# Attention stream: filled-in products in thirds, seven PSUM banks in one set, and a new order of a unit's steps

## The chip, the cores and the metric

The kernel runs on one core of a Trainium2 chip. The metric is the device time of one execution in microseconds. Three runs of the kernel before took 5718.77, 5719.36 and 5725.56 us, so the median is 5719.36 us.

## The reference

The program is a two-part encoder on x of shape (4, 2048, 256), float32 throughout.

- Part 1: `x = x + attention(layernorm(x))`. Full self-attention with 16 heads of 16 features over all 2048 positions, separately for each of the 4 batches: `softmax(Q K^T / 4 + lambda * prior) V`, then an output projection. The prior depends on the distance d of the two positions alone: `0.8 exp(-(d-1)^2/0.5) + 0.4 exp(-(d-30)^2/8)`, which the kernel takes as zero from a distance of 60 on.
- Part 2: `x = x + two local layers(layernorm(x))`. Each has windowed attention (8 heads of 64, window 128, rotary positions) and a gated feed-forward network.

The change lies in part 1, the "attention stream".

## The kernel before

**Units.** The stream has 1024 units: 4 batches x 16 heads x 16. In its first stage a unit u takes 128 queries of a head against all 2048 keys, for the largest score of every query. In its second stage, LEAD = 22 units later, a unit s takes 128 keys against all 2048 queries with the maximum already in the product, and makes exponentials and the weighted sum of values. The loop over t emits for each t the steps of `ORDER`, a list written out by hand: stage one of unit t and stage two of unit t - 22, interleaved. A prime after a step's name (`m'`) means that it is done for the unit before (t - 1). TensorE (PE), ScalarE (ACT) and VectorE (DVE) execute their instructions in just this order; while t < LEAD the shorter list `FIRST` is used.

**Steps of a unit.** Scores have 512 columns each; four make a unit in either stage. A *half* is one of the two halves of the keys; it has a left and a right score tile.

- `L`, `R` (L866): the two left and the two right products of stage one. In `R`, where a half is not touched by the prior's band (it is not `apart`), the keys are the difference right minus left (`kd`), so that max(left, right) = left + relu(difference).
- `r` (L886, ACT): relu of such a difference. `m` (L890, DVE): the maximum of left plus relu. One half of a unit is of this kind in 14 of 16 units, none in the other two.
- `dR`, `dL` (L878 plain maximum, L880 with the prior added; DVE): the maxima of a half's right and left tile where the half is `apart`. L880 is two rows of the profile, the operation and a READ_ACCUMULATOR.
- `A`, `B` (L949): two products each of stage two. `bA`, `bB` (L960, DVE): the prior's band added to the tiles that it touches. `x0` to `x3` (L964, ACT): the four exponentials, `x0` and `x1` of `A`'s tiles, `x2` and `x3` of `B`'s.
- `W` (L973): the weighted sums, eight rows of PE. `W'` takes the exponentials of the unit before.
- `F` and `E`: places for filled-in work. At most one filled-in group of products goes to PE in a unit, at `F`; what reads its result comes at `E`.

**Filled-in work.** A timetable of generators (`fillers`) runs two slots per unit, one at `F` and one at `E`. `on_pe()` yields until it is at an `F` that nobody has taken. The generators are: `projections` of the following batch (per group of four chunks: two transposes `xt`, four products `pqk` of 6 matmuls, two `pv` of 12 matmuls of half the width), `residual` of the batch before (eight transposes `oT`, eight groups `ao` of 12 matmuls), and `prepare_layers`, which prepares weights of part 2 and has 20 small groups `b_w`; it pauses while one of the other two is active (`counted`, `when_quiet`). `projections(b)` starts at unit (b-1)*256 + 60, `residual(b)` at unit (b+1)*256 + 25.

**PSUM.** Eight banks. One holds the weighted sums of a head (`pacc`). Stage one has a pool of its own of three banks (`P1 = 3`), for four tiles per unit. Stage two and the filled-in products share the other four. A product waits until the instructions that read the tile before it in its bank are done.

**DVE work per head.** Four short steps of `negated` (L898 to L909) at the steps in `BETWEEN`, and the steps of `kept_sums` (two transposes L984 and L989, a copy on ACT, a reciprocal) at `R` and `dR`.

Of the kernel before, what the change touches and what calls it, by code (L numbers as in the profile page):

```python
# [37 lines left out]
P = 128  # L38
# [22 lines left out]

ORDER = "m' R A F r dR bA x0 B E L bB x2 W' dL x1 x3".split()

FIRST = "m' R r dR bA L bB F dL E x3".split()

BETWEEN = "bA", "bB", "dL", "x3"

# [5 lines left out]
SECOND, TURN = 12, 8  # L73
PART, FULLS, MORE, P1 = 2, 4, 2, 3
Q_BUFS, V_BUFS = 6, NC + 2
# [112 lines left out]
def encoder_kernel(  # L188
# [47 lines left out]

    def prepare_layers(wp, psum, on_pe, behind):

# [21 lines left out]
        for l in range(DEPTH):  # L260
# [66 lines left out]
            for k in range(2):  # L327
                rows = l_w1[l, k * P : (k + 1) * P, :]
                for at, n in ((0, 3), (3, 2), (FULL, 3), (FULL + 3, 2), (2 * FULL, 1)):
# [20 lines left out]
                    yield from behind()  # L350
                    nc.vector.tensor_tensor(b1[:, at : at + n], b1[:, at : at + n], ps[:, :n], ALU.add)
                    nc.gpsimd.tensor_scalar(s, s, lb[:, 0, k : k + 1], None, ALU.mult)
                    yield
# [45 lines left out]

    def dense(ps, lefts, rights, last=True, first=True):  # L400

        n = len(lefts)
        for k in range(n):
            (lh, ll), (rh, rl) = lefts[k], rights[k]
            for i, (a, c) in enumerate(((lh, rh), (lh, rl), (ll, rh))):
                nc.tensor.matmul(  # L406
                    ps, a, c, start=first and k == 0 and i == 0,
                    stop=last and k == n - 1 and i == 2,
                )

# [17 lines left out]
    def attention():  # L428
        with ExitStack() as es:
# [8 lines left out]
            xp = es.enter_context(tc.tile_pool(name="ax", bufs=2))  # L438
            p1 = es.enter_context(tc.tile_pool(name="p1", bufs=P1, space=PSUM))
            p2 = es.enter_context(tc.tile_pool(name="p2", bufs=7 - P1, space=PSUM))  # L440
            pacc = es.enter_context(tc.tile_pool(name="pa", bufs=1, space=PSUM))

            def psum(name):
                return p2.tile([P, 512], F32, tag="ps", name=name)

# [113 lines left out]
            xts, keys = {}, {}  # L559
            phase = {"at": None, "taken": False}  # L560

            def on_pe():

                while phase["at"] is not None and (phase["at"] or phase["taken"]):
                    yield 1
                phase["taken"] = True

            def behind():
# [29 lines left out]
            def turned(b, g, xt):  # L598
                t = xts[b, g] = [
                    xp.tile([P, 2, QT], F32R, tag=f"xT{i}", name=f"xT{i}_{b}_{g}", bufs=XT_BUFS)  # L600
                    for i in range(2)
                ]
                for k in range(2):
                    yield from on_pe()
                    ps = psum(f"xt_{b}_{g}_{k}")
                    for i in range(4):
                        nc.tensor.transpose(
                            ps[:, i * P : (i + 1) * P], xt[:, i, k * P : (k + 1) * P], ident
                        )
                    yield from behind()  # L610
                    nc.scalar.copy(t[0][:, k], ps)
                    yield 1
                    nc.vector.tensor_tensor(t[1][:, k], ps, t[0][:, k].bitcast(F32), ALU.subtract)

            def store(queue, stack, cols, part, parts):
# [11 lines left out]
            def project_qk(b, i, m, g, given=None):  # L627
# [6 lines left out]
                feats = slice(m * P, (m + 1) * P)  # L634
                dense(
                    ps,
                    [[w[:, a, i, k, feats] for a in range(2)] for k in range(2)],
                    [[xT[a][:, k] for a in range(2)] for k in range(2)],
                )
                yield from behind()  # L640
                bias = bqk_sb[:, i, m : m + 1]
                if given:
                    nc.scalar.activation(given[0], ps, AF.Identity, bias=bias)
                    nc.vector.scalar_tensor_tensor(
                        given[1], ps, bias, given[0].bitcast(F32), ALU.add, ALU.subtract
                    )
                    if not i:
                        return
                full = qp.tile([P, QT], F32, tag="full", name=f"full_{name}", bufs=FULLS)
                nc.scalar.activation(full, ps, AF.Identity, bias=bias)  # L650
                if i:
                    keys[m, g] = full
# [69 lines left out]
            def project_v(b, g, pair):  # L722
# [3 lines left out]
                yield from on_pe()  # L726
                ps = psum(f"pv_{b}_{c}")
                for i in range(2):
                    tok = slice((2 * pair + i) * P, (2 * pair + i + 1) * P)
                    dense(  # L730
                        ps[:, i * D : (i + 1) * D],
                        [[xT[a][:, k, tok] for a in range(2)] for k in range(2)],
                        [[w[:, a, 2, k, :] for a in range(2)] for k in range(2)],
                    )
                if b:
                    both = vp.tile([P, 2, VW], F32, tag="vst", name=f"vst_{b}_{c}", bufs=2)
# [10 lines left out]
                for i in range(2):  # L747
# [5 lines left out]
                    else:  # L753

                        nc.scalar.copy(dst, src)
                        nc.gpsimd.tensor_tensor(dst, dst, bias, ALU.add)
                if b:
                    nc.sync.dma_start(scratch_v[b][c : c + 2].rearrange("c p d -> p c d"), both)
# [94 lines left out]
            def pair_of_products(u, right):  # L853
# [5 lines left out]
                for half in in_pair(u, right):  # L859
# [3 lines left out]
                    else:  # L863
                        keys = k1[h % 2][rows, right * QT : (right + 1) * QT]
                    ps = pairs[u, right, half] = p1.tile([P, QT], F32, tag="s1", name=f"s1_{u}_{right}{half}")
                    nc.tensor.matmul(  # L866
# [4 lines left out]
            def tile_max(u, right, half):  # L871
# [7 lines left out]
                else:  # L879
                    nc.vector.tensor_tensor_reduce(  # L880
                        ps, ps, prior, 1.0, LOWEST, ALU.add, ALU.max, top
                    )

            def positive(u, half):
                more = mores[u, half] = ep.tile([P, QT], F32, tag="more", name=f"more_{u}_{half}", bufs=MORE)
                nc.scalar.activation(more, pairs.pop((u, 1, half)), AF.Relu)  # L886

            def both_max(u, half):
# [3 lines left out]
                    tops[u // NC][:, chunk(u), 2 * half : 2 * half + 1],  # L892
                )

            def negated(h):
# [66 lines left out]
            def weights(s, j):  # L962
                e = es_[s, j] = ep.tile([P, QT], F32, tag="e", name=f"e_{s}_{j}")
                nc.scalar.activation(e, sums.pop((s, j)), AF.Exp)  # L964

            def weigh(s):
# [42 lines left out]
            def residual(b):  # L1009
# [22 lines left out]
                for n in range(8):  # L1032
# [21 lines left out]
                    yield 1  # L1054
                    nc.vector.tensor_tensor(rest, by_chunk, high.bitcast(F32), ALU.subtract)
                if last:
                    fetch(0)
                    fetch(1)
                for g in range(4):
                    x1 = x1s_.pop(g)  # L1060
                    oT = oTs[g]
                    for i in (0, 2):
                        yield from on_pe()
                        ps = psum(f"ao_{b}_{g}_{i}")
                        for n in range(2):
                            tok = slice((i + n) * P, (i + n + 1) * P)
                            dense(
                                ps[:, n * D : (n + 1) * D],
                                [[oT[a][:, k, tok] for a in range(2)] for k in range(2)],
                                [[w[:, a, 3, k, :] for a in range(2)] for k in range(2)],  # L1070
                            )
                        yield from behind()
                        nc.vector.tensor_tensor(
                            x1[:, i : i + 2], x1[:, i : i + 2],
                            ps.rearrange("p (c f) -> p c f", c=2), ALU.add,
                        )
                    queue.dma_start(apart_by_four(x1s[b], g), x1)
                    mv = small.tile([P, 4, 2], F32, tag="mv4", name=f"mv_f{b}_{g}")
# [136 lines left out]
            fillers.add(projections(0, ("second",)), 2 * SECOND)  # L1215
            fillers.add(when_quiet(prepare_layers(lp, psum, on_pe, behind)), 2 * (LEAD + 4), 2)
            for b in range(batches):
                if b:
                    fillers.add(
                        counted(projections(b, ("first", "second", "v"))),  # L1220
                        2 * ((b - 1) * units + PROJECT_AT), STRIDE,
                    )
                fillers.add(counted(residual(b)), 2 * ((b + 1) * units + LEAD + 3))

            def fill(t, at):
                phase["at"], phase["taken"] = at, False
                fillers.run(2 * t + at + 1)
# [5 lines left out]
            for t in range(total + LEAD + 4):  # L1233
# [12 lines left out]
                for step in ORDER if t >= LEAD else FIRST:  # L1246
                    what, u = step.rstrip("'"), t - step.count("'")
                    s = u - LEAD
                    if what in BETWEEN:
                        next(end, None)  # L1250
                    if what in ("R", "dR"):
                        done, at = divmod(t - LEAD - 1, NC)
                        if what == "R" and at == 0 and 0 < done <= batches * NH:
                            sums_end = kept_sums(done - 1)
                        next(sums_end, None)
                    if what in "RLrm" or what in ("dR", "dL"):
                        if not 0 <= u < total:
# [3 lines left out]
                        for half in range(2):  # L1261
                            if apart(u, half):
                                if what[0] == "d":
                                    tile_max(u, int(what == "dR"), half)
                            elif what == "r":
# [595 lines left out]
```

## Time and profile before

| | |
|---|---|
| median of three runs | 5719.36 us |
| the profiled execution's own time | 5719.48 us |
| its span | 5717.4 us |
| granted TensorE clock, mean | 0.99 |
| busy: PE, DVE, ACT, POOL | 95%, 85%, 78%, 38% |
| first `W` of stage two, last `W` | 128.4 us, 3033.7 us |
| part 2 (the local layers) | from about 3050 us to the end |

How to read it: the profiled execution took as long as the median run, so its rows can be set against the time. Busy shares are means over the whole program; PE's is the sum of modelled spans of matmuls, which overlap waits. The stream is the stretch from 128.4 to 3033.7 us, 1023 periods from one `W` to the next; all that the change touches lies there and in the lead-in before it. A period with no filled-in product on PE has a median of 2.61 us.

### The profile page before, as it was taken

Reading aid. Unit: us, or ns where it says so; the run is one execution under the profiler, and the core shown is the slowest. Engines: PE = TensorE matmul, PEld = TensorE weight load, DVE = VectorE, ACT = ScalarE, POOL = GpSimd, SP = SyncE. Lnnn points to the kernel's source line nnn. Section 1 sums busy time; section 2 is a strip of 40 time slices with the busy share of each in tenths; the row PEclk is TensorE's granted clock in tenths of the full one; section 3 lists DMA queues with packets and bytes.
Section 4 is the critical chain, followed back from the end, with each engine's and each line's share of the span. In section 5 each row is a group of like instructions: output and inputs, shape, how many; then the busy total and the mean of one; then the engine's idle time right before and its main releaser. Section 6 shows DMA issues by size and latency. Waiting matters only on the chain.

```text
span 5717.4 us, 105497 instructions
## 1 busy us (share of the span) xinstructions
PE 5458.9 (95%) x35544; PEld 3380.0 (59%) x35544; DVE 4834.0 (85%) x13769; ACT 4466.0 (78%) x9400; POOL 2183.5 (38%) x2368
## 2 busy tenths in 40 slices
PE   7999999999999999999997999999999999999998
PEld 4444444444444444444444787888887887888787
DVE  6888999889998899999985888888888888888886
ACT  3889998889988899889996667766776676666665
POOL 3232002311123200110003666666666666666665
PEclk8999999999999999999998999999999999999999
DMA  4444233432434422323213221212122322222211
GB/s 153 130 142 120 75 96 102 142 102 85 114 111 133 128 78 66 112 83 106 60 45 113 52 55 48 55 52 55 48 57 80 89 55 63 58 63 56 63 52 40
DMA packets 337242, 477.30 MB, mean 83 GB/s; under 512 B 67296, under 2 KB 191200, under 8 KB 335168
## 3 DMA queue, kind: packets, MB, share of 16 engines
q1 hardware_dynamic: 323744, 434.36, 27.1%
q0 software_dynamic: 12960, 36.20, 2.2%
q8 instruction: 284, 4.65, 0.3%
q14 instruction: 254, 2.08, 0.1%
HBM read 267.80 MB, written 126.09 MB: 69 GB/s over the span
## 4 chain that ended last, share of the span: by engine, by line
PE 59%; DVE 23%; ACT 9%; POOL 5%; issue 3%; DMA 2%; SPq 0%; POOLq 0%; DVEq 0%; ACTq 0%
PE s L866 16%; PE acc L973 16%; PE s L949 9%; PE w L406 4%; ACT sim L1527 4%; PE sim L1501 3%; POOL rn L375 3%; DVE s L880 3%; DVE lk L1363 2%; PE qkv L406 2%; PE po L1581 2%; DVE sim L1513 2%; DVE hn L1646 2%; DVE tops L878 2%; PE pqk L406 1%
## 5 line engine op out<-in xcount | busy, mean ns | idle before, releaser
L964 ACT ACTIVATE e<-s 128x512 f32<-128x512 f32 x4096 | 2152.7, 611 | 192.7 <-PE s L949 120.4
L866 PE MATMUL s<-k,q 64*128 64x512 f32 x3200 | 1291.8, 465 | 68.4 <-DVE tops L880 34.9
L880 DVE CUSTOM_DVE_ANT_0 s<-s,wide 128x512 f32<-128x512 f32 x1408 | 976.6, 694 | 199.5 <-PE s L866 186.5
L973 PE MATMUL acc<-e,v 128*32 128x512 f32 x8192 | 1096.0, 607 | 0.0
L949 PE MATMUL s<-q,k 64*128 64x512 f32 x4096 | 839.7, 418 | 5.4 <-issue 3.7
L866 PEld LDWEIGHTS s<-k,q 64*128 64x128 f32 x3200 | 531.1, 185 | 515.2 <-ACT more L886 255.8
L1527 ACT ACTIVATE sim<-sim,top,rn 128x256 f32<-128x256 f32 (+1 forms) x1024 | 597.3, 586 | 260.0 <-DVE top L1519 259.5
L878 DVE TENSOR_REDUCE tops<-s 128x1 f32<-128x512 f32 x896 | 610.5, 682 | 64.3 <-PE s L866 60.5
L1538 POOL TENSOR_TENSOR sim<-sim,inv 128x512 f32<-128x512 f32 (+1 forms) x512 | 512.9, 1023 | 347.2 <-DVE inv L1535 344.1
L949 PEld LDWEIGHTS s<-q,k 64*128 64x128 f32 x4096 | 540.5, 186 | 133.0 <-ACT e L964 53.7
L890 DVE CUSTOM_DVE_ANT_0 more<-s,more 128x512 f32<-128x512 f32 x896 | 614.1, 685 | 0.9 <-ACT more L886 0.6
L866 PEld LDWEIGHTS s<-kd,q 64*128 64x128 f32 x896 | 164.7, 184 | 744.3 <-DVE tops L880 378.5
L886 ACT ACTIVATE more<-s 128x512 f32<-128x512 f32 x896 | 539.9, 603 | 68.7 <-PE s L866 37.2
L406 PE MATMUL w<-gt,ww 128*128 128x512 f32 x2112 | 545.6, 397 | 3.5 <-DVE lk L1363 3.1
L960 DVE TENSOR_TENSOR s<-s,band 128x187 f32<-128x187 f32 (+2 forms) x1408 | 469.2, 354 | 65.5 <-PE s L949 64.5
L866 PE MATMUL s<-kd,q 64*128 64x512 f32 x896 | 446.3, 498 | 0.5 <-DVE tops L878 0.2
L406 PEld LDWEIGHTS w<-gt,ww 128*128 128x128 f32 x2112 | 387.4, 189 | 79.2 <-issue 3.7
L1426 POOL TENSOR_TENSOR r<-r,t 128x256 f32<-128x256 f32 x512 | 366.9, 738 | 149.5 <-DVE t L1413 140.3
L1513 DVE CUSTOM_DVE_ANT_0 sim<-sim,cst 128x256 f32<-128x256 f32 (+1 forms) x1024 | 376.6, 409 | 55.7 <-PE sim L1501 52.6
L375 POOL TENSOR_TENSOR rn<-ss,nhalf 128x16 f32<-128x16 f32 x128 | 372.7, 2912 | 95.8 <-DVE ss L374 92.9
L1004 POOL TENSOR_TENSOR oall<-o,inv 128x256 f32<-128x256 f32 x64 | 39.8, 622 | 962.7 <-DVE inv L1003 943.1
L1501 PE MATMUL sim<-lk,lq 128*128 128x256 f32 (+1 forms) x2048 | 338.6, 294 | 28.5 <-DVE lq L1363 18.8
(196 smaller groups left out, 9648.8 us busy)
## 6 DMA issues: line engine op xcount, KB each, us to landing
lk<-lk SPq DMA_DIRECT2D x256, 256.0 KB
k<-sm SPq DMA_DIRECT2D x512, 96.0 KB
q<-sm SPq DMA_DIRECT2D x508, 96.0 KB
sm<-part SPq DMA_DIRECT2D x168, 256.0 KB
q<-sm SPq DMA_DIRECT2D x128, 192.0 KB
k<-sm SPq DMA_DIRECT2D x126, 192.0 KB
fg<-f SPq DMA_DIRECT2D x32, 512.0 KB
tb<-td SPq DMA_DIRECT2D x128, 128.0 KB
```

Of the source, the lines that this page charges most:

```text
L375: nc.gpsimd.tensor_tensor(dst, var, nhalf[:, : var.shape[1]], ALU.pow)
L406: nc.tensor.matmul(ps, a, c, start=first and k == 0 and i == 0, stop=last and k == n - 1 and i == 2,)
L866: nc.tensor.matmul(ps, q1[u // 4 % Q_BUFS][rows, u % 4 * P : (u % 4 + 1) * P], keys, start=True, stop=True,)
L878: nc.vector.tensor_reduce(top, ps, AX.X, ALU.max)
L880: nc.vector.tensor_tensor_reduce(ps, ps, prior, 1.0, LOWEST, ALU.add, ALU.max, top)
L886: nc.scalar.activation(more, pairs.pop((u, 1, half)), AF.Relu)
L890: nc.vector.tensor_tensor_reduce(more, ps, more, 1.0, LOWEST, ALU.add, ALU.max, tops[u // NC][:, chunk(u), 2 * half : 2 * half + 1],)
L949: nc.tensor.matmul(ps, k2[s // 4 % Q_BUFS][rows, kc % 4 * P : (kc % 4 + 1) * P], q2[h % 2][rows, j % 2 * QT : (j % 2 + 1) * QT], start=Tru ...
L964: nc.scalar.activation(e, sums.pop((s, j)), AF.Exp)
L973: nc.tensor.matmul(acc[32 * j : 32 * j + 32, :], vs[b, kc][:, own * VS : own * VS + 32], es_.pop((s, j)), start=kc == 0, stop=kc == NC - 1,)
L1527: nc.scalar.activation(w, w, AF.Exp, bias=m["top"][:, h : h + 1], scale=s["rn"][:, h : h + 1], accum_out=m["sums"][:, h : h + 1],)
L1538: nc.gpsimd.tensor_tensor(w, w, m["inv"][:, hs].unsqueeze(2).to_broadcast([P, 2, width]), ALU.mult)
```

## The change

Three edits, all in part 1.

1. **Thirds.** A group `pqk`, `pv` or `ao` no longer goes to PE as a whole at one `F`, but in three parts (2, 2, 2 or 4, 4, 4 matmuls) at the `F` of three successive units, with its bank held from the first third to the reading of the result. While a group is open no other filled-in product may start. In the lead-in (t < LEAD) and after the stream a group still goes as a whole. `projections(b+2)` now follow `residual(b)` in one generator, where they ran at times of their own.
2. **One set of seven banks.** The pools of three and four banks become seven single-bank tiles. A list of free banks is kept when the program is written: `psum` takes the bank that has been free longest in the order of the program, and `release`, called after the last step that reads a tile, puts its bank at the end.
3. **A new order.** `x3` and `x2` of a unit move to the next unit (`x3'`, `x2'`); `m'` comes behind `F`; `dR` and `dL` are split in two (`dR1`, `dR2`: the first and, where both halves are apart, the second half), `dR2`, `bB`, `dL1` and `dL2` are at the end.

```diff
-ORDER = "m' R A F r dR bA x0 B E L bB x2 W' dL x1 x3".split()
-FIRST = "m' R r dR bA L bB F dL E x3".split()
-BETWEEN = "bA", "bB", "dL", "x3"
+ORDER = "x3' R A F m' dR1 x2' r x0 B bA L E x1 W' dR2 bB dL1 dL2".split()
+FIRST = "m' R r dR1 dR2 bA L bB F dL1 dL2 E".split()
+BETWEEN = "bA", "dR2", "bB", "dL2"
+SUMS = "R", "dR1"
+THIRDS, BANKS = 3, 7
...
-            p1 = es.enter_context(tc.tile_pool(name="p1", bufs=P1, space=PSUM))
-            p2 = es.enter_context(tc.tile_pool(name="p2", bufs=7 - P1, space=PSUM))
+            pp = es.enter_context(tc.tile_pool(name="pp", bufs=1, space=PSUM))
...
+            free, taken = list(range(BANKS)), {}
+
             def psum(name):
-                return p2.tile([P, 512], F32, tag="ps", name=name)
+                i = taken[name] = free.pop(0)
+                return pp.tile([P, 512], F32, tag=f"ps{i}", name=name)
+
+            def release(name):
+                free.append(taken.pop(name))
...
-            def on_pe():
+            def on_pe(more=False):
-                while phase["at"] is not None and (phase["at"] or phase["taken"]):
+                while phase["at"] is not None and (
+                    phase["at"] or phase["taken"] or (phase["open"] and not more)
+                ):
                     yield 1
                 phase["taken"] = True
+
+            def in_thirds(products):
+                n = len(products) // THIRDS
+                phase["open"] = True
+                for i, product in enumerate(products):
+                    if i and i % n == 0 and phase["at"] is not None and not phase["early"]:
+                        yield from on_pe(more=True)
+                    product()
+                phase["open"] = False
...
-                dense(
+                yield from in_thirds(dense_products(
                     ps,
...
-                    ps = pairs[u, right, half] = p1.tile([P, QT], F32, tag="s1", name=f"s1_{u}_{right}{half}")
+                    ps = pairs[u, right, half] = psum(f"s1_{u}_{right}{half}")
...
+                release(f"s1_{u}_{right}{half}")
...
+            def between(b):
+                yield from residual(b)
+                if b + 2 < batches:
+                    yield from counted(projections(b + 2, ("first", "second", "v")))
+
+            fillers.add(counted(projections(1, ("first", "second", "v"))), 2 * PROJECT_AT, STRIDE)
             for b in range(batches):
-                if b:
-                    fillers.add(
-                        counted(projections(b, ("first", "second", "v"))),
-                        2 * ((b - 1) * units + PROJECT_AT), STRIDE,
-                    )
-                fillers.add(counted(residual(b)), 2 * ((b + 1) * units + LEAD + 3))
+                fillers.add(between(b), 2 * ((b + 1) * units + LEAD + 3))
...
                             if apart(u, half):
-                                if what[0] == "d":
-                                    tile_max(u, int(what == "dR"), half)
+                                if what[0] == "d" and int(what[2]) == 1 + (half and apart(u, 0)):
+                                    tile_max(u, int(what[1] == "R"), half)
```

The `release` shown stands at the end of `tile_max` (`dR1` to `dL2`); others stand behind the last step that reads the tile: behind `r`, `m`, `x0` to `x3` and the steps that read a filled-in result. `dense_products` returns the list of matmuls that `dense` issued at once; the `pv` and `ao` groups collect two such lists and hand them to `in_thirds` together.

More of the change, by code (lines that the diff above doesn't have):

```diff
@@ L73 @@
 SECOND, TURN = 12, 8
-PART, FULLS, MORE, P1 = 2, 4, 2, 3
+PART, FULLS, MORE = 2, 4, 2
 Q_BUFS, V_BUFS = 6, NC + 2
@@ L235, in encoder_kernel, with prepare_layers @@
         tables.append(dp.tile([P, NC, 4, LD], F32, tag=f"td{l}", name=f"td{l}"))
-    def prepare_layers(wp, psum, on_pe, behind):
+    def prepare_layers(wp, psum, release, on_pe, behind):
         def load(dst, src):
@@ L351, in prepare_layers @@
                     nc.vector.tensor_tensor(b1[:, at : at + n], b1[:, at : at + n], ps[:, :n], ALU.add)
+                    release(f"b1_{name}")
                     nc.gpsimd.tensor_scalar(s, s, lb[:, 0, k : k + 1], None, ALU.mult)
@@ L398, in evacuate, with dense_products @@
         nc.vector.tensor_tensor(l, ps, h.bitcast(F32), ALU.subtract)
-    def dense(ps, lefts, rights, last=True, first=True):
+    def dense_products(ps, lefts, rights, last=True, first=True):
         n = len(lefts)
+        products = []
         for k in range(n):
@@ L405, in dense @@
             for i, (a, c) in enumerate(((lh, rh), (lh, rl), (ll, rh))):
-                nc.tensor.matmul(
-                    ps, a, c, start=first and k == 0 and i == 0,
+                products.append(partial(
+                    nc.tensor.matmul, ps, a, c, start=first and k == 0 and i == 0,
                     stop=last and k == n - 1 and i == 2,
-                )
+                ))
+        return products
+    def dense(*args, **kwargs):
+        for product in dense_products(*args, **kwargs):
+            product()
     def rows(t):
@@ L559, in attention @@
             xts, keys = {}, {}
-            phase = {"at": None, "taken": False}
-            def on_pe():
-                while phase["at"] is not None and (phase["at"] or phase["taken"]):
+            phase = {"at": None, "taken": False, "open": False}
+            def on_pe(more=False):
+                while phase["at"] is not None and (
+                    phase["at"] or phase["taken"] or (phase["open"] and not more)
+                ):
                     yield 1
                 phase["taken"] = True
+            def in_thirds(products):
[4 more added lines that the diff above has]
+                        yield from on_pe(more=True)
+                    product()
+                phase["open"] = False
             def behind():
@@ L613, in turned @@
                     nc.vector.tensor_tensor(t[1][:, k], ps, t[0][:, k].bitcast(F32), ALU.subtract)
+                    release(f"xt_{b}_{g}_{k}")
             def store(queue, stack, cols, part, parts):
@@ L638, in project_qk @@
                     [[xT[a][:, k] for a in range(2)] for k in range(2)],
-                )
+                ))
                 yield from behind()
@@ L647, in project_qk @@
                     if not i:
+                        release(f"pqk_{name}")
                         return
@@ L650, in project_qk @@
                 nc.scalar.activation(full, ps, AF.Identity, bias=bias)
+                release(f"pqk_{name}")
                 if i:
@@ L727, in project_v @@
                 ps = psum(f"pv_{b}_{c}")
+                products = []
                 for i in range(2):
                     tok = slice((2 * pair + i) * P, (2 * pair + i + 1) * P)
-                    dense(
+                    products += dense_products(
                         ps[:, i * D : (i + 1) * D],
@@ L734, in project_v @@
                     )
+                yield from in_thirds(products)
                 if b:
@@ L756, in project_v @@
                         nc.gpsimd.tensor_tensor(dst, dst, bias, ALU.add)
+                release(f"pv_{b}_{c}")
                 if b:
@@ L886, in positive @@
                 nc.scalar.activation(more, pairs.pop((u, 1, half)), AF.Relu)
+                release(f"s1_{u}_1{half}")
             def both_max(u, half):
@@ L893, in both_max @@
                 )
+                release(f"s1_{u}_0{half}")
             def negated(h):
@@ L964, in weights @@
                 nc.scalar.activation(e, sums.pop((s, j)), AF.Exp)
+                release(f"s2_{s}_{j}")
             def weigh(s):
@@ L1055, in residual @@
                     nc.vector.tensor_tensor(rest, by_chunk, high.bitcast(F32), ALU.subtract)
+                    release(f"oT_{b}_{g}_{k}")
                 if last:
@@ L1064, in residual @@
                         ps = psum(f"ao_{b}_{g}_{i}")
+                        products = []
                         for n in range(2):
                             tok = slice((i + n) * P, (i + n + 1) * P)
-                            dense(
+                            products += dense_products(
                                 ps[:, n * D : (n + 1) * D],
@@ L1071, in residual @@
                             )
+                        yield from in_thirds(products)
                         yield from behind()
@@ L1076, in residual @@
                         )
+                        release(f"ao_{b}_{g}_{i}")
                     queue.dma_start(apart_by_four(x1s[b], g), x1)
@@ L1215, in attention @@
             fillers.add(projections(0, ("second",)), 2 * SECOND)
-            fillers.add(when_quiet(prepare_layers(lp, psum, on_pe, behind)), 2 * (LEAD + 4), 2)
-            for b in range(batches):
-                if b:
-                    fillers.add(
-                        counted(projections(b, ("first", "second", "v"))),
-                        2 * ((b - 1) * units + PROJECT_AT), STRIDE,
-                    )
-                fillers.add(counted(residual(b)), 2 * ((b + 1) * units + LEAD + 3))
+            fillers.add(when_quiet(prepare_layers(lp, psum, release, on_pe, behind)), 2 * (LEAD + 4), 2)
+            def between(b):
[3 more added lines that the diff above has]
+            fillers.add(counted(projections(1, ("first", "second", "v"))), 2 * PROJECT_AT, STRIDE)
+            for b in range(batches):
+                fillers.add(between(b), 2 * ((b + 1) * units + LEAD + 3))
             def fill(t, at):
-                phase["at"], phase["taken"] = at, False
+                phase["at"], phase["taken"], phase["early"] = at, False, t < LEAD
                 fillers.run(2 * t + at + 1)
@@ L1250, in attention @@
                         next(end, None)
-                    if what in ("R", "dR"):
+                    if what in SUMS:
                         done, at = divmod(t - LEAD - 1, NC)
@@ L1255, in attention @@
                         next(sums_end, None)
-                    if what in "RLrm" or what in ("dR", "dL"):
+                    if what in "RLrm" or what[0] == "d":
                         if not 0 <= u < total:
```

## The prediction

> **What bounds the kernel now.** I read the busy line of the page first, then busy time by stretches, the waits of TensorE's weight loads, and the timeline of one plain and one filled unit.
>
> ```profile
> PE 5458.9 (95%) x35544; PEld 3380.0 (59%) x35544; DVE 4834.0 (85%) x13769; ACT 4466.0 (78%) x9400; POOL 2183.5 (38%) x2368
> ```
>
> ```profile
> 600.00:800.00 200.00, 197.95 (x1217) 82.00 (x1216) 182.23 (x543) 188.24 (x370) 16.19 (x31) 1.00 0.25 71
> ...
> 1000.00:1200.00 200.00, 195.81 (x1188) 89.22 (x1185) 164.08 (x489) 165.53 (x322) 65.81 (x114) 1.00 0.48 140
> ```
>
> The columns are PE, PEld, DVE, ACT, POOL, clock, DMA share, GB/s. Without projections (600 to 800) ACT and DVE are at 94% and 91%; with them (1000 to 1200) both fall to 82%: the filled-in products starve them. But the plain stretch isn't saturated either, as the waits and the timeline there show:
>
> ```profile
> PEld s L866 <- ACT more L886: 22.5, 62, 0.4
> ```
>
> ```profile
> 1503.12 0.50 PE L866 MATMUL s<-kd,q 64*128 64x512 f32 x1
> ...
> 1503.66 0.60 ACT L886 ACTIVATE more<-s 128x512 f32<-128x512 f32 x1
> ...
> 1504.31 0.18 PEld L866 LDWEIGHTS s<-k,q 64*128 64x128 f32 x1 [0.24 <-ACT more L886]
> ...
> 1504.73 1.07 PE L973 MATMUL acc<-e,v 128*32 128x512 f32 x8
> ...
> 1504.84 0.69 DVE L880 CUSTOM_DVE_ANT_0 s<-s,wide 128x512 f32<-128x512 f32 x1
> ...
> 1505.44 0.14 DVE L880 DVE_READ_ACCUMULATOR2_ANT tops<- 128x1 f32 x1
> ...
> 1505.73 0.50 PE L866 MATMUL s<-kd,q 64*128 64x512 f32 x1
> ...
> 1506.30 0.70 DVE L880 CUSTOM_DVE_ANT_0 s<-s,wide 128x512 f32<-128x512 f32 x1 [0.16 <-PE s L866]
> ```
>
> The plain period is a loop through one PSUM bank. R starts at 1503.12; `r` follows 0.54 later; it lasts 0.60; 0.05 after its end the second L product, which takes R's bank, is let go (1504.31); W' follows after 0.42, the next R after 1.00. 0.54 + 0.60 + 0.05 + 0.42 + 1.00 = 2.61 us, just the median period. PE is in order, so this wait sets everything. Own work would allow less: ACT's five operations start 0.48 to 0.49 apart (2.4 us), DVE's fill 2.3 us.
>
> A filled unit, by contrast, is bound by PE's own work:
>
> ```profile
> 317.65 0.49 PE L866 MATMUL s<-kd,q 64*128 64x512 f32 x1
> ...
> 318.31 1.66 PE L406 MATMUL pqk<-xT,aw 128*128 128x512 f32 x6
> ...
> 319.89 0.50 PE L949 MATMUL s<-q,k 64*128 64x512 f32 x2
> ...
> 320.23 0.40 PE L866 MATMUL s<-k,q 64*128 64x512 f32 x2
> 320.56 1.06 PE L973 MATMUL acc<-e,v 128*32 128x512 f32 x8
> ...
> 321.56 0.49 PE L866 MATMUL s<-kd,q 64*128 64x512 f32 x1
> ```
>
> R to R is 3.91 us, of which `pqk` takes 319.89 - 318.31 = 1.58; without it PE needs 2.33. Sorting the 1023 periods (W' to W') by what lies in them: 859 without a product (median 2.61, mean 2.67), 48 with `pqk` (mean 3.91), 24 with `pv` (3.96), 24 with `ao` (4.29), 48 with transposes (3.28 to 3.41), 20 with `b_w` (3.27). Over 2.61 the whole groups cost 48 x 1.30 + 24 x 1.35 + 24 x 1.68 = 135 us.
>
> **The change: which bank goes to whom.** With seven banks and a queue of free ones, each tile takes the bank of the seventh release before it. Per unit with one half of either kind the releases are, in order, x3', m', dR1, x2', r, x0, x1, dL1, and the tiles R R A A B B L L. At the start three are held (those of x2', x3', m'), four free (r, x0, x1, dL1 of the unit before). So R takes those of r and x0, A of x1 and dL1, B of x3' and m', and **L those of dR1 and x2' of its own unit**. The wait of L on `r` is gone; one on `dR1` has come. Behind it on PE stand W' and the next R and A, and for those wait `r` and `x0` on ACT and the next dR1 on DVE. While a filled-in bank is held, everything shifts by one: B takes m' and dR1, L takes x2' and r; then B waits for dR1. A's banks (x1, dL1 of the unit before) and F's (x3') come free before PE gets there.
>
> **Plain unit, new loop.** R to dR1's start 0.56 to 0.57 (1505.73 to 1506.30); dR1 until its accumulator is read 0.74 (1504.84 to 1505.58), or 0.69 as a plain maximum (mean of L878: 682 ns); 0.05; L to W' 0.42; W' to R 1.00. That is 0.56 + 0.74 + 0.05 + 0.42 + 1.00 = 2.77, or 2.72. By the chunks' places the right tile has the band in 9 of the 14 such units, so 2.75 on average, 0.145 over 2.61. DVE is ready for it: from L, dL1 0.56 + 0.61, m' 0.70, makes 1.87, and dR1's product is ready at 0.42 + 1.00 + 0.56 = 1.98; only 0.11 to spare. Thirds make 96 groups into 288 filled units, so 859 - 192 = 667 plain ones stay; 14/16 are of this kind: 584 x 0.145 = **+85 us**. The other 83 (two apart halves; means 2.80 and 2.93 before) hang on DVE's four maxima and stay.
>
> **Filled units.** A third is 0.53 us of PE; 2.33 + 0.53 = 2.86. The loop is longer: 0.56 + 0.74 + 0.05, then B to L 0.34 (319.89 to 320.23), L to W' 0.33, W' to R 1.00 = 3.02, or 2.97: 3.00. The third lies hidden in the wait of B. 288 x (3.00 - 2.61) = 112 against 135 before: **-23 us**. Bounds: 2.86 where B doesn't wait (-63), 3.10 where DVE is late too (+6).
>
> **Transposes and `b_w`** (68 units) hold a bank in the same way, as before: 0.4 us each either way, -27 to +27; I take 0.
>
> **DVE's other work.** A head's sums and negation (L984 449 ns, L989 441, reciprocal 250, four short ones some 770 in all: 1.9 us) and the 96 statistics of filled-in tiles (412 + 199 ns) were covered: plain units with an ACT copy of the sums have a median of 2.61 too. Now dR1 has 0.11 us to spare, and the transposes stand ahead of it. Part still fits between dR1 and dL1 (0.6 us, 0.38 of it bands). From 0 to 64 x 1.1 + 58 = 128; I take a third, **+42**, since the other places are on slack.
>
> **The rest** at nothing. The new places of `negated` put its two SP transfers at most a unit later, with six units before the second stage reads them. By the generators' yields batch 1's projections end at unit 174 (before: 126), needed at 242; batch 3's at 699, needed at 754; weights' preparation at 936 of 1024. POOL (38%) and SP have the same work, spread wider. Lead-in and tail: 22 units bound by DVE, -10 to +10.
>
> Sum: 85 - 23 + 42 = +104 on 5719.48 (the profiled execution, at the median): **5823 us**. 0.2%, 11 us, is about what a measurement here can tell.
>
> The Trainium skill speaks against the change at one place: "TensorE: Matmul & The Clock Gate", section "A second HAM failure mode: psum-queue depth-cycling", tells of products cycling through banks whose small idle times let the clock fall and rise. Here the clock is 1.00 in both stretches, though PE waits in nearly every plain unit. If one unit in ten ran at half clock, an estimate by that page is 100 x 2.3 = 230 us more; I follow the row, and the sum holds nothing of it.
>
> **Rivals.**
> - *Faster: L's bank comes free sooner* (chance 0.16). If the release came at the end of the operation's 0.60 and not with the accumulator's read, and W' followed L after 0.33 as in the filled unit, the plain loop is 0.56 + 0.60 + 0.05 + 0.33 + 1.00 = 2.54, the filled one 2.88: 584 x -0.07 + 288 x 0.27 - 135 = -98, so 5621. It decides where R to L falls below 1.19 us. For it: 0.33 is in the rows. Against: loads of L866 are let go 0.05 after READ_ACCUMULATOR's end, where they wait for it, and 0.42 is what follows a load that waited.
> - *No change* (0.12): only the 0.33 holds and DVE's other work stays covered: 584 x 0.06 = 35, less 23: 5732.
> - *DVE is the bound* (0.12): all of its other work shows, 128 in place of 42: 85 - 23 + 128 = +190, so 5909. For it: 0.11 us to spare; against: its busy share falls in a longer unit.
> - Main case: 0.60, from 5770 to 5870.
>
> **Numbers.** The range 5700 to 5910 holds the main case, the no-change case and the DVE case, 0.84 in all; it leaves out the faster rival. Faster by over 0.2%: 0.17 (the rival and a little of the unknown). Same: 0.06, half of the no-change case. Slower: 0.77, the rest.
>
> **What would show it.** Right: the waits of L866 on ACT `more` all but vanish, those on DVE `tops` hold L in each unit by some 0.2 us or more; plain periods of 2.7 to 2.8; filled ones near 3.0 with two or four matmuls in each; the last W' near 3135 us; clock still 1.00, part 2 as long as before. Wrong: plain periods at or under 2.61, or filled ones under 2.8; a clock below 1.00 in the stream; projections that come late, as waits of `k` or `q` on DMA.

## The result, and the profile after

The changed kernel takes 5843.4 us (median of four runs, 5841.4 to 5846.3), the kernel before 5719.1 us beside it: a ratio of 1.0215 (1.0203 to 1.0227). It is 124 us slower; 104 were forecast. The profiled execution has a span of 5839.8 us at a mean clock of 0.99. The last `W'` of the stream is at 3155.6 us (before: 3033.7, forecast "near 3135"); what follows it takes 2684 us in both. So the loss lies in the stream: the spans differ by 122 us, of which 117 fall between the first and the last `W'` and 4 ahead of it.

The timeline of plain units after (start us, us, engine, line, operation; `W'` is now L1011, `L` and `R` are L900, `dR1` and `dL1` are L912 and L914, `A` and `B` are L986, `r` is L921, `m'` is L926, the filled-in products are L593):

```profile
601.58 0.50 PE L900 MATMUL s<-kd,q 64*128 64x512 f32 x1
...
602.16 0.69 DVE L912 TENSOR_REDUCE tops<-s 128x1 f32<-128x512 f32 x1 [0.15 <-PE s L900]
...
602.90 0.49 PE L900 MATMUL s<-k,q 64*128 64x512 f32 x2 [0.34 <-DVE tops L912]
...
603.33 1.06 PE L1011 MATMUL acc<-e,v 128*32 128x512 f32 x8
...
604.32 0.49 PE L900 MATMUL s<-kd,q 64*128 64x512 f32 x1
...
604.89 0.70 DVE L914 CUSTOM_DVE_ANT_0 s<-s,wide 128x512 f32<-128x512 f32 x1
...
605.50 0.14 DVE L914 DVE_READ_ACCUMULATOR2_ANT tops<- 128x1 f32 x1
...
605.70 0.50 PE L900 MATMUL s<-k,q 64*128 64x512 f32 x2 [0.30 <-DVE tops L914]
```

This is the forecast loop. R at 601.58; `dR1` starts 0.58 later, lasts 0.69; both L products go together 0.05 after its end (602.90); `W'` 0.43 after that, the next R 0.99 after `W'`: 2.74 us. In the next unit `dR1` is the operation with the band, its bank comes free when the accumulator's read ends (605.64), and L goes at 605.70. The bracket on PE's rows names who let L go: `dR1`, as in nearly every plain unit (633 of 667).

The waits of TensorE's weight loads, 600 to 800 us (waited for, us in total, times, longest):

```profile
PEld s L900 <- ACT e L1001: 58.7, 70, 0.8
...
PEld s L900 <- DVE tops L914: 32.9, 49, 0.7
PE s L900 <- DVE tops L914: 17.5, 49, 0.4
...
PE s L900 <- DVE tops L912: 4.0, 13, 0.3
```

No row of L900 on ACT `more` is left, where there were 62 waits before. (The first row is the 0.84 us between the last weight load of `W'` and the first of R, in which PE is busy with `W'`; it was there before too, under DVE's name.) PE itself now waits 62 times for `tops`, some 0.35 us each.

A filled unit after, 306.95 to 309.98:

```profile
306.95 0.49 PE L900 MATMUL s<-kd,q 64*128 64x512 f32 x1
...
307.61 0.74 PE L593 MATMUL pqk<-xT,aw 128*128 128x512 f32 x2
...
308.13 0.14 DVE L914 DVE_READ_ACCUMULATOR2_ANT tops<- 128x1 f32 x1
...
308.28 0.23 PEld L986 LDWEIGHTS s<-q,k 64*128 64x128 f32 x2 [0.37 <-DVE tops L914]
...
308.61 0.44 PE L900 MATMUL s<-k,q 64*128 64x512 f32 x2
...
308.99 1.06 PE L1011 MATMUL acc<-e,v 128*32 128x512 f32 x8
...
309.98 0.50 PE L900 MATMUL s<-kd,q 64*128 64x512 f32 x1
```

As told, `dR1` now lets go `B` (308.28) and not L. The third of two matmuls lies ahead of `B` and takes 0.67 us here, so that PE is done with it just when `dR1`'s read ends (308.27). R to R is 3.03 us.

Busy time by stretches:

```profile
600.00:800.00 200.00, 175.41 (x1128) 67.62 (x1128) 174.85 (x504) 180.85 (x348) 18.51 (x40) 1.00 0.30 87
1000.00:1200.00 200.00, 190.87 (x1148) 73.74 (x1140) 174.60 (x517) 172.86 (x330) 34.39 (x58) 1.00 0.35 99
```

In the plain stretch everything has less to do per microsecond: ACT 181 of 200 (188 before), DVE 175 (182). In the filled one ACT and DVE have more (173 and 175 against 166 and 164), which is what the thirds were to do; but that stretch holds less of the filled-in work per microsecond, since a group now takes three units.

Sorting the periods from `W'` to `W'` again, in us:

| periods | before: number, mean | after: number, mean (median) |
|---|---|---|
| plain | 859, 2.67 | 667, 2.85 (2.81) |
| with a group or a third | 96, 4.02 | 288, 3.14 (3.04) |
| transposes | 48, 3.34 | 48, 3.24 |
| `b_w` | 20, 3.27 | 20, 3.09 |

Plain: 667 x (2.85 - 2.67) = +121. Groups: 904 us in 288 units, against 386 in 96 and 192 plain ones at 2.67, 898 in all: +6. Transposes and `b_w`: -5 and -4. Sum +118, the stream's loss.

### The profile page after: what moved, and what is told of

Read it like the earlier page. It is cut to its first block, busy times and chain, and to the rows that moved or that the text cites. A ratio compares the mean times of both kernels' runs of the same rounds, so it can differ in the third digit from the quotient of the medians.

```text
span 5839.8 us, 106957 instructions
## 1 busy us (share of the span) xinstructions
PE 5391.5 (92%) x35544; PEld 3256.9 (56%) x35544; DVE 4886.7 (84%) x13769; ACT 4521.1 (77%) x9400; POOL 2187.9 (37%) x2368
## 4 chain that ended last, share of the span: by engine, by line
PE 45%; DVE 31%; ACT 10%; issue 6%; POOL 5%; DMA 1%; SPq 1%; POOLq 0%; DVEq 0%; ACTq 0%
PE acc L1011 12%; PE s L900 11%; DVE s L914 7%; PE w L418 4%; PE s L986 4%; ACT sim L1572 4%; DVE tops L912 4%; PE sim L1546 3%; POOL rn L378 3%; PE qkv L418 3%; DVE lk L1408 2%; PE po L1626 2%; DVE sim L1558 2%; DVE hn L1691 2%; DVE more L926 2%
## 5 line engine op out<-in xcount | busy, mean ns | idle before, releaser
L1001 ACT ACTIVATE e<-s 128x512 f32<-128x512 f32 x4096 | 2212.2, 605 | 182.3 <-DVE s L997 76.6
L900 PE MATMUL s<-k,q 64*128 64x512 f32 x3200 | 1012.7, 476 | 222.2 <-DVE tops L914 150.9
L914 DVE CUSTOM_DVE_ANT_0 s<-s,wide 128x512 f32<-128x512 f32 x1408 | 980.1, 697 | 217.2 <-PE s L900 179.7
L1011 PE MATMUL acc<-e,v 128*32 128x512 f32 x8192 | 1096.7, 605 | 3.0 <-ACT e L1001 2.5
L986 PE MATMUL s<-q,k 64*128 64x512 f32 x4096 | 892.2, 424 | 32.6 <-DVE tops L926 15.2
L912 DVE TENSOR_REDUCE tops<-s 128x1 f32<-128x512 f32 x896 | 610.0, 687 | 113.9 <-PE s L900 100.5
L900 PEld LDWEIGHTS s<-k,q 64*128 64x128 f32 x3200 | 399.2, 185 | 535.9 <-DVE tops L914 293.1
L986 PEld LDWEIGHTS s<-q,k 64*128 64x128 f32 x4096 | 508.0, 185 | 271.4 <-DVE tops L914 86.1
L921 ACT ACTIVATE more<-s 128x512 f32<-128x512 f32 x896 | 538.1, 601 | 134.6 <-PE s L900 105.5
L926 DVE CUSTOM_DVE_ANT_0 more<-s,more 128x512 f32<-128x512 f32 x896 | 606.6, 677 | 9.5 <-ACT more L921 9.4
L900 PEld LDWEIGHTS s<-kd,q 64*128 64x128 f32 x896 | 164.9, 184 | 746.5 <-ACT e L1001 728.6
L900 PE MATMUL s<-kd,q 64*128 64x512 f32 x896 | 446.0, 498 | 7.2 <-DMA q<-sm 4.5
```

Source lines behind the costliest of these rows:

```text
L900: nc.tensor.matmul(ps, q1[u // 4 % Q_BUFS][rows, u % 4 * P : (u % 4 + 1) * P], keys, start=True, stop=True,)
L912: nc.vector.tensor_reduce(top, ps, AX.X, ALU.max)
L914: nc.vector.tensor_tensor_reduce(ps, ps, prior, 1.0, LOWEST, ALU.add, ALU.max, top)
L926: nc.vector.tensor_tensor_reduce(more, ps, more, 1.0, LOWEST, ALU.add, ALU.max, tops[u // NC][:, chunk(u), 2 * half : 2 * half + 1],)
L986: nc.tensor.matmul(ps, k2[s // 4 % Q_BUFS][rows, kc % 4 * P : (kc % 4 + 1) * P], q2[h % 2][rows, j % 2 * QT : (j % 2 + 1) * QT], start=Tru ...
L1011: nc.tensor.matmul(acc[32 * j : 32 * j + 32, :], vs[b, kc][:, own * VS : own * VS + 32], es_.pop((s, j)), start=kc == 0, stop=kc == NC - 1,)
```

## The experiments

The theory: what costs the time is that in the new order the seventh release before L is that of its own unit's `dR1`. The rivals: the one set of banks, the thirds, or DVE's load makes the difference.

**e1: the order of before, with seven banks and thirds.**

```diff
-ORDER = "x3' R A F m' dR1 x2' r x0 B bA L E x1 W' dR2 bB dL1 dL2".split()
-FIRST = "m' R r dR1 dR2 bA L bB F dL1 dL2 E".split()
-BETWEEN = "bA", "dR2", "bB", "dL2"
+ORDER = "m' R A F r dR1 dR2 bA x0 B E L bB x2 W' dL1 dL2 x1 x3".split()
+FIRST = "m' R r dR1 dR2 bA L bB F dL1 dL2 E x3".split()
+BETWEEN = "bA", "bB", "dL2", "x3"
```

Expected: 

> The changed kernel with the order of before (its steps dR and dL under their new names); seven banks in one queue and thirds stay. Theory: the time was lost to L's wait for its own unit's dR1, which comes from the new order. In the old order the seventh release before L is that of m' and r, so the plain period is the old loop of 2.61 us again; a filled unit is bound by PE's own work, 2.33 + 0.53 = 2.86, so the 288 filled units cost 72 us over 2.61 where the whole groups cost 135: about 5655 us (5630 to 5690). Rival: the queue of seven banks or the thirds cost the time and the order little: 5800 or more, plain periods at 2.75 or more.

Measured: 5677.8 us, 0.9929 of before (0.9914 to 0.9943). Plain units have a median of 2.61 again (mean 2.64), and the wait on `r` (L921) is back, 600 to 800 us:

```profile
PEld s L900 <- ACT more L921: 22.7, 60, 0.4
```

Filled units have medians of 2.98 to 2.99, not 2.86. TensorE's timeline in e1 shows why:

```profile
344.34 0.50 PE L900 MATMUL s<-kd,q 64*128 64x512 f32 x1
...
344.68 0.40 PE L986 MATMUL s<-q,k 64*128 64x512 f32 x2
345.01 0.73 PE L593 MATMUL pqk<-xT,aw 128*128 128x512 f32 x2
345.67 0.50 PE L986 MATMUL s<-q,k 64*128 64x512 f32 x2
346.01 0.39 PE L900 MATMUL s<-k,q 64*128 64x512 f32 x2
346.33 1.06 PE L1011 MATMUL acc<-e,v 128*32 128x512 f32 x8
347.33 0.50 PE L900 MATMUL s<-kd,q 64*128 64x512 f32 x1
```

No row of PE has a wait here: 2.99 us is its own work. The third, two matmuls, takes 345.67 - 345.01 = 0.66, not 1.58 / 3 = 0.53. In a whole group of six in the kernel before, the first and the last matmul take some 0.33 us each to the next start and the four between them 0.23; a third of it has only a first and a last. Three thirds are 1.98 us of PE where the whole group was 1.58. So the order alone (with its own `FIRST` and `BETWEEN`) makes 166 us of difference (5843 - 5678), and with the order of before the other two edits win.

**e2: whole groups in the changed kernel.**

```diff
-THIRDS, BANKS = 3, 7
+THIRDS, BANKS = 1, 7
```

Expected: 

> The changed kernel with whole groups (one part instead of three); order and seven banks stay. Theory: the thirds are not what costs. Plain periods stay at 2.75 to 2.80; 96 groups at some 3.95 and 192 plain units at 2.85 take 926 us, where the 288 filled units take 904 now: about 5865 us (5850 to 5890). Rival: holding a bank for three units costs the time: below 5800.

Measured: 5870.1 us (1.0263 of before, 1.0246 to 1.0280). Plain periods stay at 2.81, groups are at 3.93 to 4.02. The thirds are worth 27 us here; they don't cause the loss.

**e3: two sets of banks in the changed kernel.**

```diff
-            free, taken = list(range(BANKS)), {}
+            free, taken = [[0, 1, 2], [3, 4, 5, 6]], {}
...
-                i = taken[name] = free.pop(0)
+                i = taken[name] = free[not name.startswith("s1_")].pop(0)
...
-                free.append(taken.pop(name))
+                free[not name.startswith("s1_")].append(taken.pop(name))
```

Expected: 

> The changed kernel with its order and thirds, but banks in two queues again, three for stage one and four for the rest. Theory: it is the order and not the one set. With three banks in the order of release L's two products take the banks of m' and dR1, so the plain loop through dR1 stays at 2.72 to 2.80; in filled units the four other banks, one of them held, make B wait for x0 of its own unit (0.54 + 0.49 + 0.65 + 0.34 + 0.33 + 1.00 = 3.35): 5890 to 5940 us. Rival: the one queue of seven makes the wait: plain periods back at 2.61, 5750 or less.

Measured: 5910.7 us (1.0333, 1.0318 to 1.0349); plain median 2.80 (2.72 to 2.80 were worked out), filled 3.33 (3.35). L waits for `tops` here too, 600 to 800 us:

```profile
PEld s L900 <- DVE tops L914: 28.2, 50, 0.6
```

The wait for `dR1` comes with the order under three banks as under seven; the one set saves the changed kernel 67 us.

**e4: only the bank of `dR1` goes elsewhere.** Every engine has the same instructions in the same order; only the banks of the tiles, and with them the waits, differ. L gets the banks of `x2'` and `r`, and R gets `dR1`'s in place of `r`'s.

```diff
-                release(f"s1_{u}_{right}{half}")
+                if right and in_stream[0] and not (apart(u, 0) and apart(u, 1)):
+                    late.append(f"s1_{u}_{right}{half}")
+                else:
+                    release(f"s1_{u}_{right}{half}")
...
                             pair_of_products(u, int(what == "R"))
+                        if what == "L":
+                            for name in late:
+                                release(name)
+                            late.clear()
```

Expected: 

> The changed kernel, where in units with one apart half the bank that dR1 reads is put into the queue only behind L; nothing else differs. L then takes the banks of x2' and r. Theory: the plain loop runs through r again: 0.54 + 0.60 + 0.05 + 0.42 + 1.00 = 2.61; in a filled unit L waits for x0 of its own unit, near 3.1: 584 plain units win 0.14 to 0.2 each, 288 filled ones lose 0 to 0.1: 5740 to 5780 us. Rival: DVE or the order as such sets the plain period: within 15 us of 5843.

Measured: 5762.7 us, 1.0076 of before (1.0061 to 1.0091). The plain median is 2.61, filled ones are at 3.09. The waits, 600 to 800 us (L is L901 here, `r` L925):

```profile
PEld s L901 <- ACT more L925: 22.2, 62, 0.4
...
PEld s L901 <- DVE tops L915: 5.4, 8, 0.8
```

This is the row of before, 62 waits, in place of those on `tops`. The bank alone is worth 81 us, with the new order as it is: the plain periods together fall from 1901 to 1806 us, 95 in all. The rival, that DVE or the order as such sets the usual plain period, is out.

The bank is not all that the order costs: e4 is still 85 us above e1, which has the same seven banks and thirds. Of these, 56 us lie in the units with the copy of a head's sums (plain ones 3.48 us against 2.64 in e1). One of them in e4:

```profile
607.64 0.49 PE L901 MATMUL s<-kd,q 64*128 64x512 f32 x1
...
608.32 0.37 ACT L1029 COPY rest<-acc 128x256 f32<-128x256 f32 x1 [0.59 <-DVE o L1026]
...
609.08 0.60 ACT L925 ACTIVATE more<-s 128x512 f32<-128x512 f32 x1
```

The copy waits for DVE's transpose of the sums, and `r`, which stands behind it on ACT in the new order, starts 1.44 us after R where the plain loop has 0.54. The other 29 us were not separated.

**e5: a third order, with seven banks and thirds.**

```diff
-ORDER = "x3' R A F m' dR1 x2' r x0 B bA L E x1 W' dR2 bB dL1 dL2".split()
-FIRST = "m' R r dR1 dR2 bA L bB F dL1 dL2 E".split()
-BETWEEN = "bA", "dR2", "bB", "dL2"
+ORDER = "m' R x1' dL2' A r F dR1 x0 bA B E L bB dR2 W' x2 dL1 x3".split()
+FIRST = "m' R dL2' r dR1 dR2 bA L bB F dL1 E".split()
+BETWEEN = "bA", "bB", "dR2", "dL1"
```

Expected: 

> Seven banks and thirds with a third order: x1 and dL2 of a unit move to the next, dR1 stays behind R, L stays behind B, W' and dL1 at the end. Theory: by the seventh release L takes the banks of x1' and r, and in filled units those of r and dR1, as with the order of before; so plain periods of 2.61 and filled ones near 2.99 (PE's own work, 2.33 + 0.66): within 15 of 5678. It may win some on transposes, whose subtraction has more room. Rival (any move of x steps to the next unit costs): above 5720.

Measured: 5660.2 us, 0.9897 of before (0.9880 to 0.9913). Plain periods have a median of 2.61 as expected; the total lies 18 us under e1, three more than told. Its filled units together take 875 us where e1's take 888, and its transposes 3.07 us where e1's take 3.15. Moving these steps to the next unit costs nothing by itself. This is the fastest version measured.

**e6: a head's sums behind `dR1`.**

```diff
-SUMS = "R", "dR1"
+SUMS = "bA", "x1"
...
-                        if what == "R" and at == 0 and 0 < done <= batches * NH:
+                        if what == SUMS[0] and at == 0 and 0 < done <= batches * NH:
```

Expected: 

> The changed kernel, where the steps of a head's sums stand at bA and x1 in place of R and dR1, so that the two transposes on DVE come behind dR1 and not ahead of it. Theory: in the new order dR1 has only 0.11 us to spare, so what stands ahead of it on DVE shows in full; units with the copy of the sums (3.33 us against 2.81) fall to 2.8 to 2.95: 64 x 0.4 to 0.5 less, 5810 to 5820 us. Rival: those units are long because W' waits for the sums' bank to be read: no change, within 8 of 5843, or longer.

Measured: 5818.1 us (1.0172, 1.0157 to 1.0187), 25 less than the changed kernel. The plain units with the copy fall from 3.32 to 3.15 us in the mean, not to 2.8 to 2.95. In the changed kernel such a unit begins so:

```profile
615.55 0.50 PE L900 MATMUL s<-kd,q 64*128 64x512 f32 x1
...
615.69 0.45 DVE L1022 STREAM_TRANSPOSE o<-acc 128x256 f32<-128x256 f32 x1 [0.33 <-PE acc L1011]
...
616.65 0.69 DVE L914 CUSTOM_DVE_ANT_0 s<-s,wide 128x512 f32<-128x512 f32 x1
```

`dR1` starts 1.10 us after R, behind the transpose, which has waited for `W'`. In e6 it starts 0.56 after R in such a unit (612.77 to 613.33). What remains is another wait, as the rival had it; the waits of weight loads in e6, 600 to 1400 us:

```profile
PEld acc L1011 <- ACT rest L1025: 9.8, 17, 0.8
```

`W'` now waits for the copy of the sums on ACT, which has come later. So both held: the first transpose ahead of `dR1` did show in full, and putting it behind brings a smaller wait.

**e7: seven banks alone (order of before, whole groups).** The edit to e1 is that of e2. Like e1 and e8 it keeps the changed kernel's timetable of groups.

Expected: 

> Order of before and whole groups, with the one queue of seven banks (and the changed kernel's timetable of groups). Theory: the plain period is 2.61 as before, whole groups are bound by PE at 3.91 as before; only transposes, b_w and ao wait less for a bank, some 0.2 us in 90 units: 5695 to 5715 us. Rival: the one set is what brings e1 its gain: 5685 or less.

Measured: 5692.4 us, 0.9951 of before (0.9936 to 0.9966), 3 us under the expected range and above the rival's 5685. Plain median 2.61, `pqk` 3.91, as before; transposes 3.10 to 3.15 against 3.28 to 3.41.

**e8: thirds alone (order of before, two sets).** The edit to e1 is that of e3.

Expected: 

> Order of before and thirds, with two queues of three and four banks as before. Theory: a group then holds one of four banks for three units, so B's second product waits for x0 of its own unit in all of them: 0.54 + 0.49 + 0.65 + 0.34 + 0.33 + 1.00 = 3.35 us in 288 units, 213 us over 2.61 where whole groups cost 135: 5775 to 5805 us. Rival: thirds alone already win, the set doesn't matter: 5700 or less.

Measured: 5763.8 us, 1.0077 of before (1.0062 to 1.0092). Filled units have a median of 3.33, as worked out; the total is 11 us under the range; the plain units' mean is 2.64 where 2.67 (before) had been assumed, 20 us over 667 units. So thirds without the one set lose.

Together, medians in us:

| order | banks | whole groups | thirds |
|---|---|---|---|
| before | 3 + 4 | 5719 | 5764 |
| before | 7 | 5692 | 5678 |
| changed | 7 | 5870 | 5843 |
| changed | 3 + 4 | not run | 5911 |

The first 5719 is the kernel before, with its own timetable of groups; the other runs have the changed kernel's, and what the timetable alone does was not run. In the order of before, seven banks make the thirds useful (-14 with them, +45 without). The new order costs 147 to 178 us in each of the three places where both orders were run.

## Why the prediction was right

**The direction and its cause.** The bank that L takes, and with it the loop R, `dR1`, L, `W'`, R, was worked out from the queue of releases and is what the timeline shows; e4 takes that one bank away and the old loop of 2.61 us is back. The rival "L's bank comes free sooner" fails at the point that it named: R to L is 1.32 and 1.38 us in the two units shown, above 1.19 (by the rival's own terms, 0.56 + 0.60 + 0.05, it is 1.21). In the first, `dR1` is the plain maximum and lasts 0.69; in the second, L waits for the end of the accumulator's read. And `W'` follows L after 0.43, not 0.33. (One reading of the stretches was off, and nothing rests on it: ACT's 165.53 of 200 us with projections is 83%, not 82%.)

**Plain units, +85.** The medians by place in the head (a head has 16 units) are 2.74 or 2.81 us in most places, worked out as 2.72 and 2.77. e4 puts the bank's part at 95 us in the plain periods. The units with two apart halves stayed, as told (2.78 and 2.85 us after, 2.80 and 2.93 before).

**Filled units, -23.** This term was mis-sized: it came to +6 (with plain units of before at their mean of 2.67; against the 2.61 that the prediction used it is +18). The median is 3.04 where 3.00 was worked out, the mean 3.14. A small part is the price of a third, taken as 0.53 of PE and measured as 0.66, so that PE's own work (2.99) already exceeds the shorter loop (2.97). The larger part is the gap between mean and median, 30 us. Of it 29 lie in three of a head's 16 places: 11 in the units with the copy of the sums, 13 in those with most of the negation, 5 in the second with two apart halves. The first two, 24 us, are work that the prediction had in its next term. The lower bound given, 2.86, doesn't exist: e1, where B does not wait, stays at 2.99.

**DVE's other work, +42.** It was an estimate between 0 and 128. In plain units it is 121 - 95 = 26 us, if what e4 leaves is put down to it; the 24 in the filled ones make it 50 at most, and leave -18 for the filled units themselves. e6 gives back 25 by moving two transposes. The plain units with the copy of the sums rose from a mean of 2.63 to 3.32, those with most of the negation (the copy and the subtraction of L903 to L905, the transpose L909) from 2.75 to 3.08.

**Transposes and `b_w`, 0:** -9. **Lead-in and tail, 0:** +5, within the bounds of 10.

**The sum.** The terms came to 95 + 26 + 6 - 9 + 5 = 123 where 104 was forecast. With the 24 us where the prediction had them, each term is within 10 us of its forecast. For the +42 this is luck: it was a third of a wide estimate, with no run behind the third.

**The clock.** It is 1.00 in both stretches after, and in every other stretch of the stream from 140 to 3156 us, though PE waits some 0.3 us in nearly every plain unit. What the Trainium skill tells in "TensorE: Matmul & The Clock Gate", section "A second HAM failure mode: psum-queue depth-cycling", didn't occur here, and the 230 us estimated by it are not in the result.

The skill's page "Perfetto Trace Analysis", section "Optimization Strategy", reads a gap that repeats on an engine as a possible lack of room for the next tile. The gap here (0.34 us of PE in each plain unit) is of that kind in form, but e1 and e4 have the same seven banks and a plain period of 2.61 us: the order of release decides how long it is.

## What to carry to other kernels

With n buffers taken in the order of release, each tile waits for the n-th release before it: write that list for one unit, and look which tiles wait for a step of their own unit that itself waits for an earlier product on the same engine, since such a wait closes a loop that no engine's busy share shows. What a larger pool and finer pieces win, a new order of the steps can lose again: here they won 67 and 27 us under the changed order too, and it still ended above the kernel before. Change the order and the pool together, by that list. Splitting a group has its own price on the engine (0.13 us for each third here), to be read from the first and the last operation of a group against those between.

## What the runs showed of the hardware

- The product that takes over the bank of a VectorE operation with an accumulator was let go only at the end of the accumulator's read: 0.75 us from the operation's start, though the next operation starts after 0.61 (604.89, 605.50 and 605.64 in the plain units above). From there to the product it took some 0.05 us.
- On TensorE a run of products of one kind cost about 0.1 us at either end: the first and the last of six `pqk` matmuls take some 0.33 us to the next start, those between 0.23; a third is 0.66 us where its share of the whole is 0.53.
